# Two convolution-style attention layers: second scores behind the attention of the row ahead, and their last exp behind the first copy of the projections

## The chip, the cores and the metric

The kernel runs on one core of a Trainium2 chip. The metric is the device time of one execution in microseconds (us). The engines that matter are TensorE (PE in the profile; its weight loads are PEld), ScalarE (ACT), VectorE (DVE), GpSimd (POOL) and the queue that issues DMAs (SP). They run side by side, each through its own queue in order, and wait for one another through semaphores. TensorE writes only into PSUM[...].

## The reference

All values are fp32. The input `x` has 128 rows of 256 tokens with 256 channels. Two layers follow each other; each adds to `x` an attention of its group-normalised self. Only the first layer matters here:

```python
def layer0(x):                       # x: (1, S=128 rows, R=256 tokens, 256 channels)
    m = group_norm(x)                # 32 groups of channels, statistics over all rows and tokens
    bias = einsum('nijz,zh->nhij', pair_repr, bias_proj)        # one for all rows
    gate = sigmoid(m @ gate_proj)
    q, k, v = split(m @ qkv_proj)    # 8 heads of 32 channels
    sim = softmax(einsum('nsqhc,nskhc->nshqk', q, k) / sqrt(32)) + bias
    attend = einsum('nshqk,nskhc->nsqhc', sim, v) * gate
    return x + attend @ out_proj
```

Attention runs within a row: 256 queries against 256 keys for each of 8 heads. The bias is added after the softmax, so its product with v can be taken apart from the exponentials. Layer 1 is a banded attention with four heads of 64 channels.

## The kernel before, in words

A first stage reads the inputs, takes the statistics for the group norm and computes the bias. Then layer 0 goes through the 128 rows one by one (the loop `for s in range(S)`, L838), from about 207 us to 2100 us; layer 1 follows with loops of its own. In layer 0 a row s is worked on as follows, and the work of three neighbouring rows is interleaved:

- `scores(s, half)` (L708): for four heads, two matmuls of 32 rows of the array (contraction over the 32 channels of a head) for each head, into four tiles `sim`, then four exps on ACT (L726) into `ex`. The four heads use four strips of the array at once.
- `sum_heads(s - 1)` (L748): the sums `zs` of the exps of the row ahead (L756, from `both`, which DVE made of pairs of exps), and the product `bv` of the bias with v (L742). Both use 32 columns of the array per head, four heads at once.
- `divide(s - 1, zs)` (L764): ACT copies `zs` to `z` (L769), DVE computes `d`, which joins the gate and the reciprocal (L771, L772).
- `attend(s - 1)` (L779): the product `av` of the exps with v (L742, also 32 columns per head), then three DVE operations (L787, L788, L790) that give `at`.
- `join_tiles` (L728): DVE adds pairs of exps (L732), four times a row; `least` (L775) is a check value on DVE.
- `stretch(names, i, s - 1)` (L811): projections of a pair of rows to come, q and k in even rows, v and the gate g in odd ones, each with seven products in place of eight (class `Seven`, L557; the order is in `sevens`, L607). ACT copies each group out of PSUM (L592 the products 1 and 5, L620 the product 2 of both, L586 and L598 the others); products 3 and 6 of a projection overwrite or add to the bank that L592 reads, so they wait for it. POOL adds parts (L604, L605). The output projection `po` of the row ahead (four matmuls, L646, from `at`) is interleaved through an iterator.
- `normal(s + 4)` loads and normalises a later row (DMAs at L353), `sum_rows` prepares sums of it on POOL (L552 to L555), and `finish(s - 1)` (L793) adds `po` to the input on DVE (L801), takes statistics (L805) and stores pairs of rows (L807).
- In even rows ACT also takes the exp of the gate of the pair (L845), which waits for POOL's add at L605.

The order of TensorE, ACT and DVE is exactly the order of the code, since these engines are under `manual_schedule`. POOL's and SP's work is placed by a planner.

Two things tie the steps together. The first is PSUM: `sim` tiles, projections and `po` share one ring of five banks (`psum(banks0, "0", 5, 0)`, L341), which are taken in turn; `zs`, `bv` and `av` have one bank each. A row takes twelve banks: four and four for scores, then the first projection, the second, the twos and `po`. So the second projection takes the bank of tile 0 of the second scores, the twos that of tile 1, `po` that of tile 2, and the next row's first scores that of tile 3. The second is the array's shape: an instruction in the profile is shown as rows*columns of the array, 32*128 for scores, 128*32 for `zs`, `bv` and `av`, 128*128 for the projections. An fp32 matmul shows as two records.

Of the kernel before, what the change touches and what calls it, by code (L numbers as in the profile page):

```python
# [10 lines left out]
AF = mybir.ActivationFunctionType  # L11
# [9 lines left out]
H0, D0 = 8, 32  # L21
# [18 lines left out]
def conv_preact_kernel(  # L40
# [14 lines left out]
    nc = tc.nc  # L55
# [16 lines left out]
    def bank(which, name):  # L72
        pool, tag, bufs = ring[which]
        return pool.tile([P, 2, R], F32, tag=tag, name=name, bufs=bufs)

    def proj_bank(name):
        return bank("proj", name)

    def sim_bank(name):
        return bank("sim", name)  # L80
# [523 lines left out]
            nc.gpsimd.tensor_tensor(self.to[:, 0], self.to[:, 0], two, ALU.add)  # L604
            nc.gpsimd.tensor_tensor(self.to[:, 2:4], self.to[:, 2:4], self.mid, ALU.add)  # L605

    def sevens(pool, f, g, name, po):  # L607


        for p in (f, g):  # L610
            p.open()
            p.product(1)
            p.product(5)
            p.take("15")
        twos = proj_bank(f"p2{name}")
        two = pool.tile([P, 2, R], F32, tag="two", name=f"two{name}", bufs=2)
        f.product(2, twos[:, 0, :], first=True)
        g.product(2, twos[:, 1, :])
        if f.bias is None:
            nc.scalar.copy(two, twos)  # L620
        else:
            f.copy(two[:, 0, :], twos[:, 0, :], 0)
            g.copy(two[:, 1, :], twos[:, 1, :], 0)
        for p in (f, g):
            p.product(3)
            p.product(6)
            p.take("6")

        for n, what in ((7, "7"), (4, "34")):
            f.product(n)  # L630
            f.take(what)
            next(po, None)
            g.product(n)
            g.take(what)
        for _ in po:
            pass
        for n, p in enumerate((f, g)):
            p.add(two[:, n, :])

    def one_by_one(w, at, name, done):  # L640

        ps = proj_bank(name)
        done(ps)
        for m in range(2):
            for kt in range(2):
                nc.tensor.matmul(  # L646
                    ps[:, m, :], lhsT=w[:, kt, m * P : (m + 1) * P], rhs=at[:, kt, :],
                    start=(kt == 0), stop=(kt == 1),
                )
                yield  # L650
# [10 lines left out]
    with ExitStack() as both:  # L661
# [3 lines left out]
        quarters1 = {w: Quarters(st1, w_in_t, n * C, f"1{w}") for n, w in enumerate("qk")}  # L665
# [9 lines left out]
        with ExitStack() as lay0:  # L675
            row = lay0.enter_context(tc.tile_pool(name="row0", bufs=2))
# [31 lines left out]
            def scores(s, half):  # L708
                i, r = divmod(s, 2)
                q, k = res["q", i], res["k", i]  # L710
                sims = [sim_bank(f"sim{s}_{half}_{j}") for j in range(4)]
                for kt in range(2):
                    for j in range(4):
                        p0 = D0 * j
                        nc.tensor.matmul(  # L715
                            sims[j][:, kt, :],
                            lhsT=k[p0 : p0 + D0, 2 * r + half, kt * P : (kt + 1) * P],
                            rhs=q[p0 : p0 + D0, 2 * r + half, :],
                            start=True, stop=True,
                        )  # L720
                ex = att.tile([P, 4, 2, R], F32, tag="ex", name=f"ex{s}_{half}", bufs=4)
                both = att.tile([P, 4, R], F32, tag="both", name=f"both{s}_{half}")
                hd[s, half] = (ex, both)

                for j in range(4):
                    nc.scalar.activation(ex[:, j], sims[j], AF.Exp, scale=1.0 / math.sqrt(D0))  # L726

            def join_tiles(s, half, j):  # L728

# [45 lines left out]
            def least(s, z):  # L775
                if s >= 0:
                    nc.vector.tensor_reduce(zmin[:, s : s + 1], z, axis=AX.XY, op=ALU.min)

            def attend(s):  # L779
                if s < 0:  # L780
                    return
                (ex0, _), (ex1, _), bv0 = hd.pop((s, 0)), hd.pop((s, 1)), hd.pop(s)
                av = ps_av.tile([P, 2, R], F32, tag="av", name=f"av{s}")
                products(av, s, lambda h, kt: (ex0, ex1)[h // 4][:, h % 4, kt, :])
                z, d = hd.pop((s, "z"))
                t = att.tile([P, 2, R], F32, tag="t", name=f"t{s}", bufs=1)
                nc.vector.tensor_tensor(t, bv0, z, ALU.mult)  # L787
                nc.vector.tensor_tensor(t, av, t, ALU.add)  # L788
                at = row.tile([P, 2, R], F32, tag="at", name=f"at{s}", bufs=1)
                nc.vector.tensor_tensor(at, t, d, ALU.mult)  # L790
                st[s]["at"] = at
# [16 lines left out]
                    outs.pop(g)  # L808
                st.pop(s)

            def stretch(names, i, s):  # L811

                po = iter(())
                if s >= 0:
                    po = one_by_one(out_sb, st[s]["at"], f"po{s}", lambda ps: st[s].update(po=ps))
                if 2 * i >= S:
                    for _ in po:
                        pass
                    return
                f, g = (  # L820
                    Seven(row, quarters[w], xns[i], tss[i], f"{w}{i}", w, by_token=(w == "v")) for w in names
                )
                for w, p in zip(names, (f, g)):
                    res[w, i] = p.to
                sevens(row, f, g, f"{names}{i}", po)


            with tc.manual_schedule(engines={mybir.EngineType.PE, mybir.EngineType.Activation, mybir.EngineType.DVE}):
                for s in range(2):
                    normal(s)  # L830
                sum_rows(0)
                stretch("qk", 0, -1)
                for s in range(2, 4):
                    normal(s)
                stretch("vg", 0, -1)
                sum_rows(1)
                most1 = Most(st1, stats1, 3, 1)
                for s in range(S):  # L838
                    scores(s, 0)
                    zs = sum_heads(s - 1)  # L840
                    join_tiles(s, 0, 0)
                    divide(s - 1, zs)
                    if s % 2 == 0:
                        e = res["g", s // 2]
                        nc.scalar.activation(e, e, AF.Exp, scale=-1.0)  # L845
                    z = hd[s - 1, "z"][0] if s > 0 else None
                    rest = ((0, 2), (1, 0), (1, 2))
                    if s < S - 1:
                        scores(s, 1)
                        attend(s - 1)  # L850
                        for half, j in rest:
                            join_tiles(s, half, j)
                        least(s - 1, z)
                        if s == 4:
                            for weights in quarters1.values():
                                weights.sum()
                        if s >= S - 3:
                            most1.join(s - S + 3)
                        stretch(("qk", "vg")[s % 2], s // 2 + 1, s - 1)
                        normal(s + 4)  # L860
                        if s % 2 == 1:
                            sum_rows((s + 3) // 2)
                        finish(s - 1)
                    else:

                        scores(s, 1)
                        for half, j in rest:
                            join_tiles(s, half, j)
                        least(s - 1, z)
                        attend(s - 1)  # L870
                load1(0)
                load1(1)
                warm = proj_bank("warm")

                def keep_on(n):

                    for _ in range(n):
                        nc.tensor.matmul(warm[:, 0, :], lhsT=ident, rhs=out_sb[:, 0, :], start=True, stop=True)  # L878

                divide(S - 1, sum_heads(S - 1))  # L880
                last_z = hd[S - 1, "z"][0]
                attend(S - 1)
                for s in (S - 2, S - 1):
                    if s == S - 1:
                        keep_on(4)
                    for _ in one_by_one(out_sb, st[s]["at"], f"po{s}", lambda ps: st[s].update(po=ps)):
                        pass
                    finish(s)
                mean1, rstd1 = channel_columns(st1, most1, 1, keep_on)
                least(S - 1, last_z)  # L890
# [5 lines left out]
        with ExitStack() as lay:  # L896
            ps_av = psum(lay, "1", 4, 0)
            row = lay.enter_context(tc.tile_pool(name="row1", bufs=4))
# [3 lines left out]
            weights = [att.tile([P, 2, 2 * WROW], F32, name=f"1p{i}", bufs=1) for i in range(4)]  # L902
# [445 lines left out]
```

## Time and profile before

| what | value |
|---|---|
| median of three runs | 3237.51 us (3233.84 to 3238.58) |
| the profiled execution | 3237.33 us, of which its span (first to last instruction) is 3235.6 us |
| granted TensorE clock, mean | 0.992 |
| PE, DVE, ACT, POOL busy | 3152.0, 2677.0, 2045.6, 1689.8 us |
| exps of layer 0 (L726) | 1024 of 128x512, mean 601 ns |
| joins of exps (L732) | 512, mean 983 ns |
| reciprocals of layer 0 (L772) | 128, mean 3353 ns |

The profile is one execution. Its page gives busy times by engine, a strip of 40 time slices, the chain of work that ended last, and groups of instructions by source line. Answers of the trace give the same for a window of time, or the instructions in order of time: start (us from the span's start), duration, engine, line, operation, output<-input, shape, count, and in square brackets the idle time before it and what ended it. Matmuls are pipelined and their ends are modelled; their starts are recorded.

### The profile page before, as it was taken

The numbers are of one execution on the slowest core, as the hardware profiler recorded it, in microseconds if no ns is written. First come the engines' busy times: TensorE is split into PE (matmuls) and PEld (weight loads), VectorE is DVE, ScalarE is ACT, GpSimd is POOL, SyncE is SP. The second block draws the span as 40 slices with busy tenths as digits, with TensorE's granted clock in tenths as the row PEclk, the third lists the DMA queues.
The fourth block names the chain that finished last, engine by engine and source line by source line (L and its number), as shares of the span: only waits on it lengthen the run. The fifth ranks groups of instructions, "written<-read, shape, count | busy, mean of one in ns | idle before, by whom it ended". The sixth has DMA issues, their size and how long they took to land.

```text
span 3235.6 us, 86853 instructions
## 1 busy us (share of the span) xinstructions
PE 3152.0 (97%) x36965; PEld 2443.7 (76%) x36965; DVE 2677.0 (83%) x3539; ACT 2045.6 (63%) x4316; POOL 1689.8 (52%) x1662
## 2 busy tenths in 40 slices
PE   6799999999999999999999999999999999999997
PEld 4567777777777777777777777678888888888886
DVE  4759999999999999999999999956777777777777
ACT  4566666666666666666666666565666666666664
POOL 3034444444444444444444444277777777777775
PEclk8999999999999999999999999999999999999999
DMA  9931211111111111111111111002222222222222
GB/s 388 415 91 54 53 34 41 34 37 37 39 35 34 41 37 37 34 40 34 40 34 41 34 40 27 21 21 67 55 66 67 67 55 66 67 67 54 67 67 48
DMA packets 346331, 209.38 MB, mean 65 GB/s; under 512 B 273608, under 2 KB 339152, under 8 KB 339664
## 3 DMA queue, kind: packets, MB, share of 16 engines
q1 hardware_dynamic: 345040, 201.37, 21.7%
q8 instruction: 293, 4.80, 0.6%
q0 software_dynamic: 752, 2.36, 0.2%
q14 instruction: 102, 0.84, 0.1%
q10 hardware_dynamic: 144, 0.00, 0.0%
HBM read 136.59 MB, written 67.11 MB: 63 GB/s over the span
## 4 chain that ended last, share of the span: by engine, by line
PE 92%; DMA 4%; DVE 3%; ACT 0%; issue 0%; POOL 0%; SPq 0%; DVEq 0%; ACTq 0%
PE sim L715 8%; PE av L742 7%; PE p1v L954 7%; PE 1po L646 7%; PE po L646 7%; PE bv L742 7%; PE pv L581 6%; PE pq L577 6%; PE p1q L577 5%; PE pk L577 5%; PE p1k L577 5%; PE pg L577 5%; PE zs L756 4%; DMA xs<-in_x_dram 3%; PE 1sim L975 3%; PE 1avz L1007 2%
## 5 line engine op out<-in xcount | busy, mean ns | idle before, releaser
L1035 DVE RECIPROCAL 1rz<-1z 128x512 f32<-128x512 f32 x128 | 427.9, 3343 | 312.2 <-ACT 1z L1029 312.2
L726 ACT ACTIVATE ex<-sim 128x512 f32<-128x512 f32 x1024 | 527.3, 601 | 249.7 <-PE sim L715 249.7
L732 DVE TENSOR_TENSOR both<-ex 128x512 f32<-128x512 f32 x512 | 483.6, 983 | 76.6 <-ACT ex L726 76.5
L772 DVE RECIPROCAL d<-d 128x512 f32<-128x512 f32 x128 | 429.2, 3353 | 4.4
L604 POOL TENSOR_TENSOR v<-v,twovg 128x256 f32<-128x256 f32 x64 | 72.9, 1139 | 551.1 <-ACT twovg L620 551.1
L715 PE MATMUL sim<-q,k 32*128 32x256 f32 x4096 | 295.7, 401 | 1.1 <-ACT ex L726 1.1
L646 PE MATMUL po<-at,out_sb 128*128 128x256 f32 x1024 | 284.6, 381 | 4.2 <-DVE at L790 4.2
L646 PE MATMUL 1po<-1at,w_out_t 128*128 128x256 f32 x1024 | 268.5, 386 | 2.9 <-DVE 1at L1041 1.8
L715 PEld LDWEIGHTS sim<-q,k 32*128 32x128 f32 x4096 | 186.4, 184 | 102.7 <-issue 69.5
L742 PE MATMUL av<-ex,v 128*32 128x256 f32 x4096 | 247.6, 382 | 0.0
L742 PE MATMUL bv<-bias_sb,v 128*32 128x256 f32 x4096 | 244.5, 379 | 0.7 <-DVE t L787 0.7
L985 POOL TENSOR_TENSOR 1p<-1ex,seen 128x768 f32<-128x768 f32 x128 | 232.7, 1818 | 23.6 <-ACT 1ex L983 23.6
L954 PEld LDWEIGHTS p1v<-w_in_t,1xn 128*64 128x64 f32 x4096 | 222.3, 137 | 21.6 <-issue 21.6
L954 PE MATMUL p1v<-w_in_t,1xn 128*64 128x128 f32 x4096 | 237.7, 274 | 0.3 <-PE warm L878 0.3
L646 PEld LDWEIGHTS 1po<-1at,w_out_t 128*128 128x128 f32 x1024 | 189.1, 190 | 51.4 <-ACT 1z L1029 22.3
L646 PEld LDWEIGHTS po<-at,out_sb 128*128 128x128 f32 x1024 | 185.4, 191 | 25.5 <-issue 4.2
L604 POOL TENSOR_TENSOR q<-q,twoqk 128x256 f32<-128x256 f32 x64 | 47.2, 737 | 298.6 <-ACT twoqk L620 298.6
L742 PEld LDWEIGHTS av<-ex,v 128*32 128x32 f32 x4096 | 120.3, 109 | 108.0 <-issue 42.1
L742 PEld LDWEIGHTS bv<-bias_sb,v 128*32 128x32 f32 x4096 | 133.2, 110 | 88.7 <-issue 1.1
L697 DVE TENSOR_SCALAR xn<-xt,mean,rstd 128x256 f32<-128x256 f32 x256 | 197.0, 809 | 0.0
L605 POOL TENSOR_TENSOR 1q<-1q,mid1q 128x512 f32<-128x512 f32 x64 | 81.7, 1277 | 189.0 <-ACT 1q L601 189.0
L992 POOL TENSOR_TENSOR 1zp<-1p 128x512 f32<-128x512 f32 x128 | 162.6, 1271 | 10.1
(263 smaller groups left out, 7664.0 us busy)
## 6 DMA issues: line engine op xcount, KB each, us to landing
pr<-in_L_conv_pair_repr_dram SPq DMA_DIRECT2D x32, 1024.0 KB, 23.0
x<-o SPq DMA_DIRECT2D x64, 512.0 KB, 2.9
yg<-x SPq DMA_DIRECT2D x64, 512.0 KB, 4.1
out_dram<-1o SPq DMA_DIRECT2D x256, 128.0 KB, 4.1
xg<-in_x_dram SPq DMA_DIRECT2D x252, 128.0 KB, 3.1
xs<-in_x_dram SPq DMA_DIRECT2D x15, 2048.0 KB, 21.7
xs<-in_x_dram SPq DMA_DIRECT2D x2, 1024.0 KB, 17.6
qkv_sb<-in_L_conv_qkv_proj_dram POOLq DMA_DIRECT2D x4, 192.0 KB, 11.5
```

The costliest lines, as they stand in the source:

```text
L577: nc.tensor.matmul(out, lhsT=weights, rhs=moving, start=first, **flags)
L581: nc.tensor.matmul(out[:, cols], lhsT=moving[:, cols], rhs=weights, start=first and t2 == 0, **flags)
L646: nc.tensor.matmul(ps[:, m, :], lhsT=w[:, kt, m * P : (m + 1) * P], rhs=at[:, kt, :], start=(kt == 0), stop=(kt == 1),)
L697: nc.vector.tensor_scalar(xns[i][:, 2 * r + half, :], xt[:, half, :], mean0[:, half : half + 1], rstd0[:, half : half + 1], op0=ALU.subtra ...
L715: nc.tensor.matmul(sims[j][:, kt, :], lhsT=k[p0 : p0 + D0, 2 * r + half, kt * P : (kt + 1) * P], rhs=q[p0 : p0 + D0, 2 * r + half, :], sta ...
L726: nc.scalar.activation(ex[:, j], sims[j], AF.Exp, scale=1.0 / math.sqrt(D0))
L732: nc.vector.tensor_tensor(both[:, j : j + 2], ex[:, j : j + 2, 0, :], ex[:, j : j + 2, 1, :], ALU.add)
L742: nc.tensor.matmul(to[D0 * j : D0 * (j + 1), half, :], lhsT=v[:, 2 * r + half, c0 : c0 + D0], rhs=weights(4 * half + j, kt), start=(kt == ...
L772: nc.vector.reciprocal(d, d)
L954: nc.tensor.matmul(ps[KB * half : KB * (half + 1), b, :], lhsT=xns[i][:, 2 * r + kt, KB * b : KB * (b + 1)], rhs=w_in_t[:, kt, 2 * C + P * ...
L985: nc.gpsimd.tensor_tensor(p.rearrange("p j (r c) -> p (j r) c", c=WROW)[:, :, 0 : 2 * WSTEP] .rearrange("p r (t c) -> p r t c", c=WSTEP)[: ...
L1035: nc.vector.reciprocal(st[s]["rz"], st[s]["z"])
```

## The change

In every row but the last, `attend(s - 1)` moves ahead of `scores(s, 1)`, and `stretch` moves ahead of the joins, `least` and `most1.join`. `scores` no longer issues its last exp itself: it issues three and returns a function for the fourth. First scores call it at once. Second scores hand it to `stretch`, which hands it to `sevens`, where it is called behind the first projection's copy of products 1 and 5 (L592). Where there is no projection left (row 126), it is called ahead of `po`.

```diff
-    def sevens(pool, f, g, name, po):
+    def sevens(pool, f, g, name, po, rest=lambda: None):
         for p in (f, g):
...
             p.take("15")
+            if p is f:
+                rest()
...
-                for j in range(4):
-                    nc.scalar.activation(ex[:, j], sims[j], AF.Exp, scale=1.0 / math.sqrt(D0))
+                def weigh(js):
+                    for j in js:
+                        nc.scalar.activation(ex[:, j], sims[j], AF.Exp, scale=1.0 / math.sqrt(D0))
+
+                weigh(range(3))
+                return lambda: weigh((3,))
...
-            def stretch(names, i, s):
+            def stretch(names, i, s, rest=lambda: None):
...
                 if 2 * i >= S:
+                    rest()
                     for _ in po:
                         pass
                     return
...
-                sevens(row, f, g, f"{names}{i}", po)
+                sevens(row, f, g, f"{names}{i}", po, rest)
...
                 for s in range(S):
-                    scores(s, 0)
+                    scores(s, 0)()
...
                     if s < S - 1:
-                        scores(s, 1)
                         attend(s - 1)
+                        last_exp = scores(s, 1)
+                        if s == 4:
+                            for weights in quarters1.values():
+                                weights.sum()
+                        stretch(("qk", "vg")[s % 2], s // 2 + 1, s - 1, last_exp)
                         for half, j in rest:
                             join_tiles(s, half, j)
                         least(s - 1, z)
-                        if s == 4:
-                            for weights in quarters1.values():
-                                weights.sum()
                         if s >= S - 3:
                             most1.join(s - S + 3)
-                        stretch(("qk", "vg")[s % 2], s // 2 + 1, s - 1)
                         normal(s + 4)
...
                     else:
-                        scores(s, 1)
+                        scores(s, 1)()
```

## The prediction

> **What bounds the kernel now.** I read the page's first and fourth parts first, to see which engine sets the end.
>
> ```profile
> PE 3152.0 (97%) x36965; PEld 2443.7 (76%) x36965; DVE 2677.0 (83%) x3539; ACT 2045.6 (63%) x4316; POOL 1689.8 (52%) x1662
> ...
> PE 92%; DMA 4%; DVE 3%; ACT 0%; issue 0%; POOL 0%; SPq 0%; DVEq 0%; ACTq 0%
> ```
>
> TensorE (PE) is busy for 97% of the span and makes up 92% of the chain. The change touches layer 0's row loop only, so next I read stretches inside that loop (columns: PE, weight loads, DVE, ACT, POOL busy; granted clock; DMA share; GB/s).
>
> ```profile
> 500.00:1000.00 500.00, 500.00 (x5261) 366.14 (x5260) 468.13 (x543) 325.17 (x661) 217.93 (x203) 1.00 0.15 37
> 1000.00:1500.00 500.00, 500.00 (x5258) 366.08 (x5257) 467.53 (x543) 324.93 (x661) 220.38 (x204) 1.00 0.15 37
> ```
>
> PE is busy all of it, DVE 94%, ACT 65%. The modelled ends of matmuls can hide waits, so I take starts only. Third view: PE's own timeline of one even row.
>
> ```profile
> 1004.52 1.15 PE L715 MATMUL sim<-q,k 32*128 32x256 f32 x16
> 1005.60 1.07 PE L756 MATMUL zs<-both,ones 128*32 128x256 f32 x16
> 1006.48 1.91 PE L742 MATMUL bv<-bias_sb,v 128*32 128x256 f32 x32
> 1008.32 1.15 PE L715 MATMUL sim<-q,k 32*128 32x256 f32 x16
> 1009.40 1.93 PE L742 MATMUL av<-ex,v 128*32 128x256 f32 x32
> 1011.26 0.70 PE L577 MATMUL pq<-xn,qkv_sb 128*128 128x256 f32 x2
> ```
>
> The reader is to see the array shapes: 32*128 (scores), 128*32 (sums, bias products, attention), 128*128 (projections). Second scores stand between two blocks of the same shape, 128*32. Instruction by instruction, an even row takes 14.71 us and an odd one 14.82 us, the same to a few ns in nearly all rows from 222 to 2071 us: TensorE waits for nobody there. A gain can only come from PE itself, a loss from a new wait of PE.
>
> **What the Trainium skill says.** "TensorEngine Tiling (Array Packing)", Key Properties: changing the tiling mode, not just the tile, drains TensorE. The trace agrees: within a block of four abreast, steps start 0.216 us apart; across scores/sums, scores/attention, attention/projections, projections/scores and bias products/scores it is 0.304 to 0.309 us. "ScalarE: Activation LUTs", What ACT_TABLE_LOAD costs: ACTIVATEs back to back overlap by about 93 ns. Here an exp of 128x512 takes 0.60 us and the next starts after 0.478 to 0.494, an overlap of some 0.12; I use the trace. "Perfetto Trace Analysis", Tensor Engine Instruction: an instruction's recorded start lies after its semaphore wait, and a LDWEIGHTS can be pulled ahead of running matmuls. The trace agrees: a projection's first weight load carries the wait and starts 0.21 us ahead of its matmul, so that load's start is the deadline for whatever frees its bank.
>
> **Part 1: one array switch fewer (the gain).** Before: sums+bias | scores | attention | projections. After: sums+bias+attention | scores | projections. No matmul is added or removed. From first weight load to first weight load, in the median row, sums+bias (48 records four abreast, 12 steps) take 2.728 us, and attention (32 records, 8 steps) 1.864 us. From 12p+h = 2.728 and 8p+h = 1.864: p = 0.216 per step, h = 0.136 us for entering and leaving a block. Joined, one h falls away: 0.136 us per row. Scores keep their 1.076 us if the hand-over scores/projections costs what scores/attention does. The trace of before has none in steady state; from both sides: 0.216 us (no drain) to about 0.40 (twice the extra), against 0.304. I take 0.304, since the five transitions above lie within 5 ns, and layer 1's 64*64 to 128*128 takes 0.306; the ends move the sum by -11 and +12 us.
>
> Rows that gain: those with an attention and a projection stretch behind it, s = 1 to 125. Row 0 has no attention; row 126 has no projections and waits 3.38 us for DVE's `at` (L790) in any order; row 127 is unchanged. 125 x 0.136 = 17.0 us.
>
> **Part 2: exps now run into the projections.** Let T be the stretch's first weight load. Second scores start at T-1.076; the first exp starts 1.164 us after them, so at T+0.088, the next at 0.582 and 1.059 (pitches 0.494, 0.477). The moved line puts the first projection's copy (L592) third: it starts at 1.54 (before: 1.169 even, 1.197 odd rows) and takes 0.586. The fourth exp starts at 2.02, the second copy at 2.50 (before 2.033, 2.062), the copy of the twos (L620) at 2.98 (before 2.896, 2.941). The mid copies (L586) were due at 3.759 and 3.887 anyway: ACT has caught up. ACT has no other instruction queued between.
>
> Who waits for that? The ring has five banks in fixed order, so each release has a deadline. ACT to PE takes 0.050 to 0.052 us where PE did wait at the start.
> - Second projection takes the bank of score tile 0: free at 0.088+0.599+0.051 = 0.738; its load starts at 0.755 (even) or 0.888 (odd). Margin 0.017 us, the thinnest.
> - Twos take tile 1's bank: free at 1.22, wanted at 1.618.
> - Product 3 of the first overwrites what the first copy reads: free at 1.54+0.586+0.051 = 2.18; wanted at 2.482 or 2.527.
> - Product 3 of the second: 2.50+0.586+0.051 = 3.14; wanted at 3.345 or 3.522.
> - `po` takes tile 2's bank: free at 1.71, wanted at 4.640. Next row's first scores take tile 3's: free at 2.68, wanted at 7.968.
>
> So PE waits 0. Were the fourth exp left ahead of the first copy, that copy would end at 2.02+0.586+0.051 = 2.65, 0.17 (even) or 0.13 us (odd) too late, and nearly all of part 1 would be gone: this part earns nothing, it keeps PE's cover.
>
> **Part 3: what is moved past what.** On DVE the order stays: scores and stretch hold no DVE instruction, so the joins (L732), `least` and `most1.join` follow attention as before. Only when their inputs land changes: the fourth exp ends at T+2.64, in row time 6.60+2.64 = 9.24 us; the joins start at 10.36 (1014.88 less 1004.52). Cost 0; this cover would be gone with exps 1.1 us later. DVE's `at` ends 10.44 us into an even row; `po` now wants it at 6.60+4.64 = 11.24 (was 11.38): margin 0.80. In odd rows DVE runs on from the even row without a break, and its margin shrinks from 1.25 to some 1.0. DVE's two waits in an even row (0.90 for exps, 0.97 for z, 1.87 us in two rows) shrink by 0.27: still idle, not the bound.
> On POOL, the weights' sums of s = 4 and the memsets of `most1.join` keep or loosen their place; adding the twos (L604) starts up to 0.09 us later, with POOL idle at least 4.7 us ahead of it. SP's order of loads (L353) and stores (L807) isn't moved and no DMA is added. The gate's exp (L845) ends 5.53 us into an even row; second scores' first exp now comes at 6.70 and no longer waits behind it.
>
> **Sum.** Profiled execution: 3237.33 us, of which the span is 3235.6 and 1.7 lies around it. 3237.3 - 17.0 = 3220.3. The median of the runs, 3237.51, is 0.2 above that execution, so 3220.5 there. I say 3220.4, a gain of 0.53%. The measurement can tell about 0.2%, 6.5 us, from no change.
>
> **Rivals.**
> 1. The new hand-over 32*128 to 128*128 is dearer, or the margin of 0.017 us is missed by a little. For: that pair of shapes isn't measured, and the margin is thin. Against: the other transitions agree within 5 ns, and the exps' starts repeat to 1 ns. At 0.09 us more per row: +11.3, so 3232, within noise of no change. If only even rows miss by 0.1 us, 62 x 0.1 = 6.2, 3227.
> 2. DVE takes over as bound. For: 94% busy, continuous over one row and a half. Against: its waits for PE are 1.87 us in two rows and `at` has 0.8 us to spare. Then PE waits out what it saved: 3237.
> 3. Slower: second scores' first exp comes late in even rows because ACT sits in the gate's exp (L845), which waits for POOL's last add (L605). POOL's order isn't written by hand; a planner could put that add behind more of the row sums (L552 to L555). The first exp is free of it by 6.70 less (5.53 - 0.10) = 1.27 us, so an add displaced by one row sum (1.18) costs nothing. Beyond that, the second projection waits 1:1 in 62 even rows. Gain gone at 0.27 us past the margin, slower by over 0.2% from 0.38 us; with a displacement of 1.8 us, 62 x 0.5 = 31 - 17 = +14: 3251. Against: the change gives the planner no new POOL work.
> 4. The order isn't what the text says: hardly, since PE, ACT and DVE are under a hand-written schedule here. I give it nothing of its own.
>
> **Chances.** Forecast 0.80; rival 1 0.09 (half of it within 0.2%); rival 2 0.05; rival 3 0.06. Faster 0.86 (forecast, half of rival 1, some of rival 2), same 0.08, slower 0.06. The likeliest case's own range is 3216 to 3225; the range on record takes in the ends of the unmeasured hand-over but for the outermost, 3211 to 3231.
>
> **What would show it.** Right: in PE's timeline bv and av run without a break, an even row's starts are 14.58 us apart and an odd one's 14.68; from second scores to projections 1.08; no wait of `pk` or `pg` on ACT; ACT's order exp, exp, exp, copy, exp. Wrong: weight loads of `pk` held by `ex` (margin missed); scores to projections over 1.1 us (dearer hand-over); `po` held by `at` (DVE); the gate's exp ending past 6.7 us of the row (rival 3).

## The result, and the profile after

The changed kernel takes 3221.15 us (median of 5 runs, 3219.68 to 3221.78) against 3238.52 us before: a ratio of 0.9949, with a 95% interval of 0.9934 to 0.9963. The time fell by 17.4 us; the forecast was 3220.4 us.

The page's first and fourth parts, of the kernel after:

```profile
PE 3135.4 (97%) x36965; PEld 2456.0 (76%) x36965; DVE 2657.6 (83%) x3539; ACT 2015.2 (63%) x4316; POOL 1693.7 (53%) x1662
...
PE 92%; DMA 4%; DVE 3%; issue 0%; POOL 0%; ACT 0%; SPq 0%; DVEq 0%; ACTq 0%; POOLq 0%
```

PE has as many instructions as before and is busy for 16.6 us less; it still carries 92% of the chain. The two stretches inside layer 0's loop (columns as before: PE, weight loads, DVE, ACT, POOL busy; clock; DMA share; GB/s):

```profile
500.00:1000.00 500.00, 500.00 (x5298) 373.30 (x5300) 468.18 (x550) 319.17 (x666) 222.95 (x206) 1.00 0.15 37
1000.00:1500.00 500.00, 500.00 (x5326) 373.05 (x5322) 465.98 (x547) 320.61 (x669) 223.82 (x208) 1.00 0.15 38
```

PE is again busy all the time, but gets through some 1% more instructions in the same 500 us. PE's own timeline of an even row shows where:

```profile
998.74 1.15 PE L717 MATMUL sim<-q,k 32*128 32x256 f32 x16
999.82 1.07 PE L763 MATMUL zs<-both,ones 128*32 128x256 f32 x16
1000.71 1.91 PE L749 MATMUL bv<-bias_sb,v 128*32 128x256 f32 x32
1002.43 1.91 PE L749 MATMUL av<-ex,v 128*32 128x256 f32 x32
1004.27 1.15 PE L717 MATMUL sim<-q,k 32*128 32x256 f32 x16
```

`zs`, `bv` and `av` are one block of shape 128*32. It goes from 999.82 to 1004.27, 4.45 us; before, its two parts took 2.73 and 1.86. Instruction by instruction, the first record of `av` follows the last of `bv` after 0.196 us, which is what two successive steps within a block show too (0.216 us from step to step, less the 0.02 us by which the four records abreast are staggered). It is not that `av` and `bv` share their weights `v`: `zs`, with other weights, hands over to `bv` in 0.196 us as well, before and after. Where there were five switches in a row there are four, each with 0.304 to 0.309 us between steps. The new one, scores to projections, has 0.304 us. In the median, even rows are 14.573 us apart (before 14.711) and odd rows 14.678 (before 14.816): 0.138 us less for both.

The view of waits for the kernel before offers another cause for the gap ahead of the projections, and so for the gain: it puts that idle time of the weight loads down to ACT (total, times, longest).

```profile
PEld pv L581 <- ACT ex L726: 25.9, 63, 0.4
PEld pq L577 <- ACT ex L726: 25.5, 62, 0.4
```

It is not one. `pq` takes the bank of tile 3 of the first scores, and in the even row of the prediction their exps had ended at 1007.75 (1005.68 + 2.07), 3.5 us before that load (1011.26):

```profile
1005.68 2.07 ACT L726 ACTIVATE ex<-sim 128x512 f32<-128x512 f32 x4 [1.33 <-PE sim L715]
```

The gap between steps there, 0.309 us, is also the same as from bias products to scores.

Weight loads and then ACT, from the first load of the same row's projections on, in the kernel after:

```profile
1005.35 0.30 PEld L577 LDWEIGHTS pq<-xn,qkv_sb 128*128 128x128 f32 x2 [0.33 <-issue]
1005.67 0.41 PEld L577 LDWEIGHTS pq<-ts,sums_q 128*128 128x128 f32 x2
1006.10 0.41 PEld L577 LDWEIGHTS pk<-xn,qkv_sb 128*128 128x128 f32 x2
```

```profile
1005.44 1.57 ACT L730 ACTIVATE ex<-sim 128x512 f32<-128x512 f32 x3 [1.15 <-PE sim L717]
1006.88 0.60 ACT L592 COPY q<-pq 128x512 f32<-128x512 f32 x1
1007.35 0.64 ACT L730 ACTIVATE ex<-sim 128x512 f32<-128x512 f32 x1
1007.84 0.63 ACT L592 COPY k<-pk 128x512 f32<-128x512 f32 x1
```

ACT's order is exp, exp, exp, copy, exp, as intended, and the load of `pk` waits for nothing.

The sum of the rows s = 1 to 125 fell by 17.2 us. Row 126 took 0.4 us longer, what follows it 0.3 less, and the profiled execution reached its first full row 1.5 us later than that of before; its span is therefore only 15.5 us shorter. That start follows from the input stage, which the change doesn't touch, and from row 0: the first scores came 1.7 us later and row 0 took 0.2 us less. In the executions below, the first scores start anywhere from 207.9 to 209.5 us, and row 0 takes from 11.5 us, where TensorE was granted its full clock (1.00), to 14.9 us, where for some 10 us the clock fell to between 0.55 and 0.77. This spreads single executions by some 3 us, so the rows are the finer measure here.

### The profile page after: what moved, and what is told of

The parts are those of the page before. It is cut to its first block, busy times and chain, and to the rows that moved or that the text cites. A ratio compares the mean times of both kernels' runs of the same rounds, so it can differ in the third digit from the quotient of the medians.

```text
span 3220.1 us, 86853 instructions
## 1 busy us (share of the span) xinstructions
PE 3135.4 (97%) x36965; PEld 2456.0 (76%) x36965; DVE 2657.6 (83%) x3539; ACT 2015.2 (63%) x4316; POOL 1693.7 (53%) x1662
## 4 chain that ended last, share of the span: by engine, by line
PE 92%; DMA 4%; DVE 3%; issue 0%; POOL 0%; ACT 0%; SPq 0%; DVEq 0%; ACTq 0%; POOLq 0%
PE sim L717 8%; PE p1v L962 7%; PE 1po L648 7%; PE po L648 7%; PE av L749 7%; PE bv L749 7%; PE pv L581 6%; PE pq L577 6%; PE pk L577 5%; PE p1q L577 5%; PE pg L577 5%; PE p1k L577 5%; PE zs L763 4%; DMA xs<-in_x_dram 4%; PE 1sim L983 3%; PE 1avz L1015 2%
## 5 line engine op out<-in xcount | busy, mean ns | idle before, releaser
L730 ACT ACTIVATE ex<-sim 128x512 f32<-128x512 f32 x1024 | 547.6, 605 | 429.8 <-PE sim L717 429.8
L749 PEld LDWEIGHTS av<-ex,v 128*32 128x32 f32 x4096 | 133.2, 110 | 87.8 <-issue 0.3
L699 DVE TENSOR_SCALAR xn<-xt,mean,rstd 128x256 f32<-128x256 f32 x256 | 179.7, 741 | 0.0
```

Of the source, the lines that this page charges most:

```text
L699: nc.vector.tensor_scalar(xns[i][:, 2 * r + half, :], xt[:, half, :], mean0[:, half : half + 1], rstd0[:, half : half + 1], op0=ALU.subtra ...
L749: nc.tensor.matmul(to[D0 * j : D0 * (j + 1), half, :], lhsT=v[:, 2 * r + half, c0 : c0 + D0], rhs=weights(4 * half + j, kt), start=(kt == ...
```

## The experiments

The theory to be tested: the time falls by the price of one array switch per row, and the place of the last exp only keeps TensorE from waiting. The rivals: the order of ACT's work is what pays; the attention's early place is what pays, through DVE; even rows alone pay, where the second exps no longer stand behind the gate's exp. All runs are compared with runs of the kernel before on the same chip; the edits are against the changed kernel.

**All four exps ahead of the first copy.**

```diff
-                weigh(range(3))
-                return lambda: weigh((3,))
+                weigh(range(4))
+                return lambda: None
```

> The changed order, but all four exps of the second scores ahead of the first copy of the projections. Theory (one array switch fewer, and the exp's place only keeps TensorE covered): the switch is still saved, but the first copy now ends 2.01 + 0.60 + 0.05 = 2.66 us after the first weight load of the projections, where product 3 wants the bank at 2.48 (even rows) or 2.53 (odd): TensorE waits 0.18 and 0.13 us. 62 x 0.18 + 63 x 0.13 = 19 us on top of 3221: 3240, no gain left over before (3238.5). In the trace the rows' starts are 14.86 (even) and 14.81 (odd) us apart. Rival (the gain is the switch alone, the exp's place doesn't matter): 3221.

Measured: 3229.89 us, before 3238.32, ratio 0.9974 (0.9965 to 0.9983). Half of the gain is left, against none in the theory and all in the rival. Weight loads and then ACT in an even row of this run:

```profile
1008.75 0.30 PEld L577 LDWEIGHTS pq<-xn,qkv_sb 128*128 128x128 f32 x2 [0.33 <-issue]
...
1011.43 0.30 PEld L577 LDWEIGHTS pq<-xn,sums_q 128*128 128x128 f32 x2 [0.23 <-ACT q L592]
```

```profile
1008.84 2.06 ACT L730 ACTIVATE ex<-sim 128x512 f32<-128x512 f32 x4 [1.16 <-PE sim L717]
1010.76 0.62 ACT L592 COPY q<-pq 128x512 f32<-128x512 f32 x1
```

The wait is where it was expected: the load of product 3 (`xn,sums_q`) is held until the first copy (L592) ends at 1011.38, and starts 2.684 us after the first load, 0.202 late (odd rows 0.156). But the rows are only 0.094 us (even) and 0.049 (odd) longer than in the changed kernel. In each, some 0.107 us of lateness costs nothing. The loads of that pair show why: a load in steady state starts with the step ahead of it, 0.216 us before its own matmul, but the two loads of the late pair start only 0.108 us apart (together they take 0.30 us in place of 0.41), so a load seems to need just half of the step. 62 x 0.094 + 63 x 0.049 = 8.9 us, close to the 8.7 measured (3229.9 less 3221.2).

**The last exp's place alone.** Attention goes back behind the second scores; the rest stays as in the changed kernel.

```diff
-                        attend(s - 1)
                         last_exp = scores(s, 1)
+                        attend(s - 1)
```

> The other part alone: second scores again ahead of the attention, but their last exp behind the first copy. Theory: five switches a row as before, and no wait on either side, so 3238.5 within 3 us, rows 14.71 and 14.82 us apart. Rival (ACT's order is what pays: an earlier first copy lets TensorE go on sooner): below 3232.

Measured: 3237.73 us, before 3238.32, ratio 1.0000 (0.9991 to 1.0008); rows 14.711 and 14.816 us apart, as before. The exp's new place earns nothing by itself, and ACT's order alone is ruled out as the source.

**Attention in halves around the scores.** `products` is given the halves to work on, and the second scores are called between them.

```diff
-                        attend(s - 1)
-                        last_exp = scores(s, 1)
+                        last_exp = attend(s - 1, lambda: scores(s, 1))
...
-                products(av, s, lambda h, kt: (ex0, ex1)[h // 4][:, h % 4, kt, :])
+                products(av, s, lambda h, kt: (ex0, ex1)[h // 4][:, h % 4, kt, :], (0,))
+                between = between()
+                products(av, s, lambda h, kt: (ex0, ex1)[h // 4][:, h % 4, kt, :], (1,))
```

> The changed kernel, but the attention's second half of heads (16 of 32 records) behind the second scores: five switches a row again, while sums, bias and half of the attention run on without a break. Theory (the number of switches decides, not where the scores stand): +0.137 us a row, 125 x 0.137 = 17 us, 3238. Rival 1 (what pays is that the attention comes early, for DVE): about half of the gain, 3230. Rival 2 (the scores being last ahead of the projections costs something that the saved switch hides): below 3238, since the exps get 1.0 us more room: 3233 or less.

Measured: 3238.56 us, before 3238.32, ratio 0.9996 (0.9988 to 1.0005). The whole gain is gone, though half of the attention is still early. PE's timeline of an even row:

```profile
1006.14 1.15 PE L717 MATMUL sim<-q,k 32*128 32x256 f32 x16
1007.22 1.07 PE L763 MATMUL zs<-both,ones 128*32 128x256 f32 x16
1008.10 1.91 PE L749 MATMUL bv<-bias_sb,v 128*32 128x256 f32 x32
1009.83 1.05 PE L749 MATMUL av<-ex,v 128*32 128x256 f32 x16
1010.81 1.15 PE L717 MATMUL sim<-q,k 32*128 32x256 f32 x16
1011.88 1.07 PE L749 MATMUL av<-ex,v 128*32 128x256 f32 x16
1012.88 0.48 PE L577 MATMUL pq<-xn,qkv_sb 128*128 128x256 f32 x1
```

`sim` stands between two blocks of 128*32 again, five switches, and rows are 14.711 and 14.816 us apart, to the nanosecond those of before. The four steps that went behind the scores cost 1.001 us there (1011.88 to 1012.88), against 0.863 for four steps within a block. What counts is the number of switches, not where the attention stands.

**Odd rows only.**

```diff
-                        attend(s - 1)
-                        last_exp = scores(s, 1)
+                        if s % 2:
+                            attend(s - 1)
+                        last_exp = scores(s, 1)
+                        if s % 2 == 0:
+                            attend(s - 1)
```

> The new order of scores and attention in odd rows only (the last exp stays behind the first copy in all rows). Theory: 63 of 125 rows save 0.137 us: 3238.5 - 8.6 = 3229.9; odd rows' starts 14.68 us apart, even rows' 14.71. Rival (the gain comes from even rows, where the second exps no longer stand behind the gate's exp): 3238.

Measured: 3230.09 us, before 3238.38, ratio 0.9975 (0.9966 to 0.9984); odd rows 14.678 us apart, even rows 14.711. Half of the rows, half of the gain: 63 x 0.138 = 8.7 us. The gate's exp, which runs in even rows only, has no part in it.

**The last exp behind the second copy.**

```diff
-            if p is f:
+            if p is g:
                 rest()
```

> The changed kernel with the last exp behind the second copy of the projections in place of the first. Theory: the first copy stays at 1.54 us, the second can start as it was before (2.03 to 2.06), the exp at 2.5, the copy of the twos at 2.98 as now; every deadline of TensorE is still met, so 3221 within 2 us. Rival (ACT's lateness at the second copy costs TensorE something now): below 3219.

Measured: 3220.59 us, before 3238.38, ratio 0.9946 (0.9932 to 0.9960), rows 14.574 and 14.678 us apart. The second copy moves from 2.49 to 2.04 us after the first load (even rows), and PE takes no notice. There was nothing left to earn on ACT.

**Tiles 1 and 0 exchanged on ACT.** This was to delay the bank that the second projection takes.

```diff
-                weigh(range(3))
+                weigh((1, 0, 2))
```

> The changed kernel with tiles 1 and 0 of the scores in swapped order on ACT, so that tile 0, whose bank the second projection takes, is free one exp later: at 0.58 + 0.59 + 0.05 = 1.22 us after the first weight load, wanted at 0.755 (even) or 0.888 (odd). Theory: TensorE waits 0.47 and 0.34 us a row, 62 x 0.47 + 63 x 0.34 = 50.5 us, 3221 + 50 = 3271; rows 15.04 and 15.02 us apart, with weight loads of pk and pg held by ex. Rival (the release of that bank has slack that the weight loads' starts don't show): 3221 to 3235.

Measured: 3219.61 us, before 3238.32, ratio 0.9946 (0.9933 to 0.9960). None of the expected 50 us came. Weight loads and then ACT in an even row:

```profile
1002.59 0.30 PEld L577 LDWEIGHTS pq<-xn,qkv_sb 128*128 128x128 f32 x2 [0.33 <-issue]
...
1003.35 0.41 PEld L577 LDWEIGHTS pk<-xn,qkv_sb 128*128 128x128 f32 x2
```

```profile
1002.70 1.57 ACT L730 ACTIVATE ex<-sim 128x512 f32<-128x512 f32 x3 [1.17 <-PE sim L717]
1004.15 0.60 ACT L592 COPY q<-pq 128x512 f32<-128x512 f32 x1
```

The exps start nearly as before (0.105, 0.599, 1.077 us after the first load), tile 1 first, and the load of the second projection starts at 0.755 without a wait, while tile 0 is read until 1.19. So the second projection doesn't wait for tile 0 here. The profile shows no banks, but the built programs do: in this one, the second projection has tile 1's bank in every row and the twos have tile 0's, while in the changed kernel it is the other way round. The banks of the ring are handed out in the order in which ACT's reads free them, not in a fixed turn; the two agree as long as ACT reads tile 0 first. The edit therefore delayed no bank that the second projection needs, and it says nothing of that bank's deadline. The next run tests the deadline.

**Tile 0 held for one more copy.** An extra copy on ACT reads tile 0 behind its exp and writes to a tile that DVE overwrites later. The second projection has tile 0's bank in this program.

```diff
-                weigh(range(3))
+                weigh((0,))
+                if half:
+                    nc.scalar.copy(both[:, 0:2], sims[0])
+                weigh((1, 2))
```

> The changed kernel, with an extra copy of score tile 0 of the second scores on ACT (into a tile that DVE overwrites later) behind its exp, so that its bank comes free at 0.565 + 0.60 + 0.05 = 1.22 us after the first weight load of the projections. The second projection's weight load starts at 0.755 (even rows) and 0.888 (odd). Theory after the first runs (a load can start up to 0.109 us late, the gap between a load of 0.107 and a step of 0.216, before its matmul is late; in odd rows v's half matmuls, 0.11 apart, leave nothing): even rows lose 0.465 - 0.109 = 0.36, odd 0.33; 62 x 0.36 + 63 x 0.33 = 43 us, 3264. As I had predicted (a load late is a matmul late): 62 x 0.465 + 63 x 0.33 = 50 us, 3271. Rival (the second projection doesn't take tile 0's bank, as the run with swapped exps could be read): 3221 to 3226.

Measured: 3267.82 us, before 3237.5, ratio 1.0092 (1.0077 to 1.0107). ACT and then the weight loads of an even row:

```profile
1023.17 0.60 ACT L730 ACTIVATE ex<-sim 128x512 f32<-128x512 f32 x1 [1.44 <-PE sim L717]
1023.66 0.58 ACT L734 COPY both<-sim 128x512 f32<-128x512 f32 x1
```

```profile
1023.40 0.41 PEld L577 LDWEIGHTS pq<-ts,sums_q 128*128 128x128 f32 x2
1024.29 0.30 PEld L577 LDWEIGHTS pk<-xn,qkv_sb 128*128 128x128 f32 x2 [0.48 <-ACT both L734]
```

The second projection's load is held by that copy (L734), until 0.051 us after its end. It starts at 1.212 in place of 0.755, 0.457 late, and the rows are 0.349 us (even) and 0.319 (odd) longer: even rows lose the lateness less 0.108, odd rows nearly all of theirs (1.213 less 0.888, 0.325). 62 x 0.349 + 63 x 0.319 = 41.7 us in layer 0, as the mended theory had it. The other 5 us of the 46.7 lie in layer 1, which took 1119.3 us from its first scores to the end, in place of 1114.2. Its ACT, DVE and POOL instructions stand in the same order there; why it took longer stays open.

**Tile 0's exp in two halves.**

```diff
-                weigh(range(3))
+                if half:
+                    for kt in range(2):
+                        nc.scalar.activation(ex[:, 0, kt], sims[0][:, kt], AF.Exp, scale=1.0 / math.sqrt(D0))
+                    weigh((1, 2))
+                else:
+                    weigh(range(3))
```

> The changed kernel with the exp of score tile 0 of the second scores as two exps of 256 columns each, so that its bank comes free some 0.08 us later, at about 0.82, and ACT is 0.07 us later behind it. Theory with the allowance: in even rows the second projection's weight load starts about 0.06 us late, at 0.82, but nothing behind it moves: 3221 within 2 us. Without the allowance: 62 x 0.06 = 4 us, 3225, even rows 14.64 us apart in place of 14.57.

Measured: 3220.14 us, before 3237.5, ratio 0.9945 (0.9932 to 0.9959). Weight loads of an even row:

```profile
1004.76 0.30 PEld L577 LDWEIGHTS pq<-xn,qkv_sb 128*128 128x128 f32 x2 [0.33 <-issue]
1005.09 0.41 PEld L577 LDWEIGHTS pq<-ts,sums_q 128*128 128x128 f32 x2
1005.56 0.36 PEld L577 LDWEIGHTS pk<-xn,qkv_sb 128*128 128x128 f32 x2
1005.95 0.41 PEld L577 LDWEIGHTS pk<-ts,sums_k 128*128 128x128 f32 x2
```

The pair of loads of `pk` starts at 0.798 in place of 0.755, 0.043 us late, and takes 0.36 us in place of 0.41; the pair behind it starts on time, and even rows stay at 14.573 us. A load can be late without its matmul being late.

## Why the prediction was right, and where it was not

**What bounds the kernel.** Right. TensorE waits for nobody in the loop before or after, and nearly all rows keep to a few nanoseconds.

**Part 1, one switch fewer: 125 x 0.136 = 17.0 us.** Right, with 0.138 us a row and 17.2 in the sum of those rows. That the median came within 0.8 us of the forecast is in part luck, since the executions of one kernel spread by 2 to 8 us. The halves put the switch back and the gain was gone; odd rows alone gave half. The unmeasured hand-over from scores to projections was taken at 0.304 us and measured 0.304. The Trainium skill's statement ("TensorEngine Tiling (Array Packing)", Key Properties) that a change of mode drains the array agrees with these runs: 0.088 to 0.093 us above a step of 0.216 in going out of a block, and the rest of the 0.138 in going in, where the first weights are not loaded ahead. The price was read from blocks of shape 128*32, and it was a block of this shape that fell away. It would not have done for another shape: a block of scores takes 1.076 us for four steps of 0.216, which is 0.21 us more than its steps.

**Row 126.** Roughly right. It gains nothing, since `po` waits for DVE's `at` (3.52 us in place of 3.38). The 0.4 us that it lost were not foreseen. They lie in `po` itself: behind the wait TensorE's granted clock falls, in the execution after to 0.51 over all eight records of `po` (steps of 0.427 us), in that of before to 0.59 over `po` and 0.81 over the scores behind it, which run at 1.00 after. That gives 0.3 of the 0.4 us back.

**Part 2, ACT's times.** Right to within 0.03 us: exps at 0.088, 0.582 and 1.060, first copy 1.537 (forecast 1.54), last exp 2.003 (2.02), second copy 2.494 (2.50), twos 2.958 (2.98); PE waits 0.

**Part 2, the deadlines.** Wrong in size, though it cost the forecast nothing. The step "that load's start is the deadline for whatever frees its bank" made the margin at the second projection 0.017 us in even rows. A load between full steps can be 0.107 us later than it is without its matmul being late (0.202 late cost 0.094 in the first run, 0.043 cost nothing in the last), so the margin was about 0.12. For the same reason "nearly all of part 1 would be gone" with four exps ahead of the first copy was wrong: half of it would, and did. In odd rows, where the load of `pg` comes behind half matmuls of `pv` (128 columns in place of 256), 0.112 us apart, the load is all but the whole step; there a late load is a late matmul. The Trainium skill ("Perfetto Trace Analysis", Tensor Engine Instruction) says that a load can be pulled ahead; I had read from this that it must be, and nothing in the trace of before showed that.

**Part 2, whose bank.** Right for this kernel, where the second projection has tile 0's bank, but for a reason that doesn't hold in general: the ring has no fixed order, the bank freed first is taken first, and with tile 1 read first it was tile 1's.

**Part 3, work moved past other work.** Right in that nothing on DVE holds TensorE: `at` comes 0.79 us (even rows; forecast 0.80) and 1.13 us (odd; forecast 1.0) ahead of `po`. Wrong in one term: DVE's waits were to shrink by 0.27 us in two rows, and they did not (0.90 and 0.96 us in an even row, before 0.90 and 0.97). What shrank is DVE's work: the four normalisations of two rows (`xn`, L697, now L699) take 752 ns each in the mean in place of 824, 0.29 us less in all. Why they do was not tested; it fits the odd rows' margin, which is larger than forecast.

**The rivals.** None came true. A dearer hand-over is excluded by 0.304 us; DVE as the bound by its margin; the gate's exp by the first exp of the second scores, which waits for PE's scores and not for ACT in even rows too.

## What to carry to other kernels

Where TensorE is busy all the time and no wait stands out, count how often neighbouring blocks change the array's shape, and put blocks of one shape together; the price can be read from two blocks of the same shape and different length in the trace. Such a move shifts the reads of PSUM against what needs their banks, so write the other engine's times beside each weight load that waits, and let the order of a single read keep the cover. A load's recorded start need not be its deadline: here, the step less the load's own time was to spare.

## What the runs showed of the hardware

One block of shape 128*32 more or less in a row costs 0.138 us in this kernel beyond its steps; a block of scores, of shape 32*128, has 0.21 us beyond its steps. The gap between the last step of one shape and the first of the next is 0.304 to 0.309 us for each of the transitions in layer 0's loop, whichever shapes are concerned. A weight load of 128 columns that is held by a semaphore can start 0.107 us late in a stream of steps of 0.216 us at no cost, and costs 1:1 beyond (0.043 us late cost nothing, 0.156 cost 0.049, 0.202 cost 0.094, 0.457 cost 0.349). Between steps of 0.112 us nearly all of the lateness is lost (0.325 us late cost 0.319). ACT's copies L592 and L622 of 128x512, which in the changed kernel follow one another and an exp without a gap, are recorded with 0.60 to 0.65 us, against 0.59 before with a gap ahead of them, while the starts stay 0.46 to 0.49 us apart.
